# Four graph layers on one core: x added in layer 4, large counts searched where A is made, the flag read between the layers

## The chip, the core and the metric

The kernel runs on one core of one Trainium2 chip. The metric is the time of one execution on the device in microseconds; the median of the runs counts. A core has these engines: PE (TensorE, with its weight loads shown apart as PEld), DVE (VectorE), ACT (ScalarE), POOL (GpSimd) and SP (SyncE), and 16 DMA engines that carry what SP, ACT and POOL issue. PE writes its results to PSUM, from which DVE and ACT read them.

## The reference

x has 6250 rows of 256. There are 100,000 edges, sorted by destination, and the destinations crowd at the low rows (6250 times the square of a uniform number); sources are uniform.

```python
h = jnp.maximum(_layernorm(x, axis=-1), 0.0)
# one network of four graph layers (h[src] summed or maximised over dst):
h = _sage_mean(h, ...)   # h @ W1_self + mean(h[src]) @ W1_neigh + b1        (256 -> 512)
h = _sage_pool(h, ...)   # h @ W2_self + max(relu(h @ W2_pool + b)[src]) @ W2_neigh + b2
h = _sage_gcn(h, ...)    # (sum(h[src]) + h) / (deg + 1) @ W3_neigh + b3
h = _sage_mean(h, ...)   # h @ W4_self + mean(h[src]) @ W4_neigh + b4
out = x + (h @ W_fc + b_fc)
```

## The kernel before

**Tiles.** The 6250 rows are 49 tiles of 128 (the last has 106). The first 18 tiles, where most edges end, are "hub" tiles (`HUB = (8, 16, 18)`: 8 are hubs in layer 1, 16 in layer 3, 18 in layer 4). For a hub tile d the kernel makes a matrix A of counts (128 sources x 49 source tiles x 128 destinations, stored as fp8 in the table tab_a), and its sum over edges is then a dense product of A with the whole source table. For the other tiles the edges are gathered in order, 128 rows at a time, and summed by products with one-hot matrices. Tables hold float32 values as three bfloat16 parts (hi, mid, lo), so that each product is three matmuls.

**Making A** (`build`). A tile has 16 windows of 8 destinations, 288 windows in all. For each group of 128 edges of a window, ACT makes a one-hot hs of the source row (L303, L305), DVE a one-hot hm of source tile and destination (L307), and PE adds their product into a PSUM bank pb of 392 columns (L313; 781 products, two banks). After the last group ACT copies the bank to A as fp8 (L317), and after 16 windows SP stores A to tab_a. The first 8 tiles are made in layer 1, where `sums` steps through its list; tiles 8 to 15 are made in the loop of layer 2 up to its step 250, tiles 16 and 17 after that.

**Layer 2** is a loop over 782 steps: POOL gathers 128 rows of tab_p (L1137), DVE takes a running maximum along the sorted edges (L1142), SP stores the runs. Between the steps the loop advances the making of A, early products for layer 3, and `done2`, which ends a tile of layer 2 (L1076, L1080) and stores its rows to tab_r. A scheduler sets the order on each engine from the program's dependences.

**Layers 3 and 4** have the same form: `sums` walks the groups of edges of the tiles that are no hubs (POOL gathers into ring, L379; DVE makes one-hots, L375; PE pg, L397; DVE accumulates, L414 and L416), and between the steps advances a list of dense products for the hub tiles (`dense`, PE pd, L435). Their A arrives in chunks of up to seven source tiles through `stream`: ACT's queue issues the loads ac (L1214), four ahead, in five buffers. A tile that is finished is handed to `done3` or `done4`, generators that `sums` steps, one step per 128 edges.

`done3` makes q = (sum + own row) / (deg + 1) + a constant row, with 512 columns (the weights that follow are already in the table's values): the first 256 are all that layer 4 needs of the row itself, the last 256 are what layer 4 sums over edges. The last 256 are split into three parts (`parts`, L280 to L283: ACT, DVE, ACT, DVE) and stored to tab_s. The first 256 are added to the rows of x, which ACT's queue has loaded (xrf), and stored to the table xq (L1280 and the line after it).

`done4` loads its tile of xq on ACT's queue (xr4, three buffers, L1303), DVE adds the sum times 1/deg (L1305), SP stores to out (L1307).

**The check and the flag.** A count of 16 or more must not go unseen: in layer 4, `stream` is called with check set, and after each load of ac DVE compares the chunk with 16, sums the hits in the same instruction (L1219) and keeps the maximum in a column of bad (L1221). Together with other checks of the input, bad is reduced after layer 4 (worst, L59), summed over the rows by PE (L63), made an integer (oddI, L67) and read into a register on all engines; if it isn't zero, a general version of the whole computation runs. It isn't run on this input.

Of the kernel before, what the change touches and what calls it, by code (L numbers as in the profile page):

```python
# [9 lines left out]
F32 = mybir.dt.float32  # L10
BF16 = mybir.dt.bfloat16
# [4 lines left out]
ALU = mybir.AluOpType  # L16
AX = mybir.AxisListType
PSUM = bass.MemoryType.PSUM
DRAM = bass.MemoryType.DRAM

P = 128
# [28 lines left out]
@with_exitstack  # L50
def kernel(ctx, tc, *aps):
    nc = tc.nc
    keep = ctx.enter_context(tc.tile_pool(name="keep", bufs=1))
    bad = keep.tile([P, 8 + MERGED], F32, name="bad")
    nc.vector.memset(bad, 0.0)
    fast_path(tc, bad, *aps)
    with tc.tile_pool(name="fl", bufs=1) as fp, tc.tile_pool(name="flp", bufs=1, space=PSUM) as pp:
        worst = fp.tile([P, 1], F32, name="worst")
        nc.vector.tensor_reduce(worst, bad, AX.X, ALU.max)  # L59
        ones = fp.tile([P, P], F32, name="ones_f")  # L60
        nc.vector.memset(ones, 1.0)
        pw = pp.tile([P, 1], F32, name="pw_f")
        nc.tensor.matmul(pw, ones, worst, start=True, stop=True)  # L63
        odd = fp.tile([P, 1], F32, name="odd")
        nc.vector.tensor_scalar(odd, pw, 1.0, None, op0=ALU.min)
        oddI = fp.tile([P, 1], I32, name="oddI")
        nc.vector.tensor_copy(oddI, odd)  # L67
        general = nc.values_load(oddI[:1, :1], min_val=0, max_val=1)
    with tc.If(general > 0):
        general_path(tc, *aps)  # L70


@with_exitstack
def fast_path(
    ctx, tc, bad, x, src, dst,
    W1_self, W1_neigh, b1, W2_pool, b2_pool, W2_self, W2_neigh, b2,
    W3_neigh, b3, W4_self, W4_neigh, b4, W_fc, b_fc, out,
):
# [11 lines left out]
    nc = tc.nc  # L90
# [115 lines left out]
    nc.vector.memset(one, 1.0)  # L206
    first_p = const.tile([P, P], F32, name="first_p")
    nc.vector.tensor_scalar(first_p, pidx.to_broadcast([P, P]), 0.0, None, op0=ALU.is_equal)

    lim = const.tile([1, 4, NT], F32, name="lim")  # L210

# [79 lines left out]
    def build(d, A, keys, pool, psb):  # L291

        sk, mk, r0 = keys
        work = []
        for w in range(d * WT, (d + 1) * WT):
            hold = {}
            for k in range(k_of[w]):
                r = row_of[w, k] - r0
                hots = {}

                def hot(r=r, hots=hots):
                    t = pool.tile([P, P], BF16, name="ht", bufs=3)
                    nc.scalar.activation(t, iota_b, AF.Abs, bias=sk[:, r : r + 1])  # L303
                    hots[0] = pool.tile([P, P], BF16, name="hs", bufs=LOOK + 3)
                    nc.scalar.activation(hots[0], t, AF.Relu, bias=one, scale=-1.0)  # L305
                    hots[1] = pool.tile([P, NT * WIN], BF16, name="hm", bufs=LOOK + 3)
                    nc.vector.tensor_scalar(hots[1], iota_w, mk[:, r : r + 1], None,  # L307
                                            op0=ALU.is_equal)

                def run(k=k, w=w, hots=hots, hold=hold):  # L310
                    if k == 0:
                        hold[0] = bank(psb, "pb", "pb", (NT * WIN,))
                    nc.tensor.matmul(hold[0], hots[0], hots[1], start=(k == 0),  # L313
                                     stop=(k == k_of[w] - 1))
                    if k == k_of[w] - 1:
                        c = (w % WT) * WIN
                        nc.scalar.copy(A[:, :, c : c + WIN],  # L317
                                       hold[0].rearrange("p (s c) -> p s c", c=WIN),
                                       saturate=True)
                        if w % WT == WT - 1:  # L320
                            nc.sync.dma_start(tab_a[d], A.bitcast(BF16))

                work.append((hot, run))
        return work
# [614 lines left out]
    with tc.tile_pool(name="fl2c", bufs=1) as ck, ExitStack() as late:  # L939
# [259 lines left out]
                    now.remove(g)  # L1199
        early.advance(len(early.work))  # L1200


    def stream(pool, chunks, check):

        got = {}
        where = {(d, s): i for i, (d, s0, s1) in enumerate(chunks) for s in range(s0, s1)}

        def load(i):
            if i >= len(chunks):
                return  # L1210
            d, s0, s1 = chunks[i]
            got[i] = pool.tile([P, 7, P], F8, name="ac", bufs=5)
            t = got[i][:, : s1 - s0, :]
            nc.scalar.dma_start(t.bitcast(BF16), tab_a[d, :, s0:s1, :])  # L1214
            if check:

                m = pool.tile([P, 1], F32, name="am")
                many = pool.tile([P, 7, P], BF16, name="many", bufs=1)
                nc.vector.tensor_scalar(many[:, : s1 - s0, :], t, 16.0, 0.0, op0=ALU.is_ge,  # L1219
                                        op1=ALU.add, accum_out=m)  # L1220
                nc.vector.tensor_tensor(bad[:, 3:4], bad[:, 3:4], m, op=ALU.max)  # L1221

        for i in range(4):
            load(i)

        def block(d, s):
            i = where[d, s]
            if s == chunks[i][1]:
                load(i + 4)
            return got[i][:, s - chunks[i][1], :]  # L1230

        return block
# [7 lines left out]
    with ExitStack() as on:  # L1240
# [8 lines left out]
        with tc.tile_pool(name="fl3", bufs=2) as wk:  # L1249
            def done3(d, acc):  # L1250
                q = wk.tile([P, FH], F32, name="q", bufs=2)
                if d < H3:
                    nc.vector.tensor_add(q, acc, acc3[d])
                    nc.vector.scalar_tensor_tensor(q, q, rgcn[:, d : d + 1], qrow,
                                                   op0=ALU.mult, op1=ALU.add)
                else:
                    if d in Z3:
                        z = Z3[d]
                    else:
                        z = wk.tile([P, 3 * FH], BF16, name="zown", bufs=2)  # L1260
                        nc.sync.dma_start(z, tab_r[d * P : (d + 1) * P, :])
                        yield 1
                        yield 1
                        yield 1
                    own = bank(psm, "pm", "pm_own")
                    for part in range(3):
                        nc.tensor.matmul(own, ident_b, z[:, part * FH : (part + 1) * FH],  # L1267
                                         start=(part == 0), stop=(part == 2))
                    yield 1
                    nc.vector.tensor_add(acc, acc, own)  # L1270
                    nc.vector.scalar_tensor_tensor(q, acc, rgcn[:, d : d + 1], qrow,
                                                   op0=ALU.mult, op1=ALU.add)
                n = P if d < NFULL else NREM
                xr = wk.tile([P, FI], F32, name="xrf")
                nc.scalar.dma_start(xr[:n, :], x[d * P : d * P + n, :])
                q3 = wk.tile([P, 3 * FO], BF16, name="q3")
                parts(q[:, FO:], FO, q3)
                nc.sync.dma_start(tab_s[d * P : (d + 1) * P, :], q3)
                yield 1
                nc.vector.tensor_add(xr[:n, :], xr[:n, :], q[:n, :FO])  # L1280
                nc.sync.dma_start(xq[d * P : d * P + n, :], xr[:n, :])
                yield 1
                for s0, s1 in z4_early:
                    if d == s1 - 1:
                        Z4.update(resident(zk, tab_s, FO, s0, s1))
# [2 lines left out]
            Z3 = {}  # L1288
            for s0, s1 in late:
                Z3.update(resident(wk, tab_r, FH, s0, s1))  # L1290
            block = stream(wk, [(d, s0, s1) for d in range(H3) for s0, s1 in late], False)
            todo = []
            work = []
            for d in range(H3):
# [1 line left out]
                              lambda acc, d=d: todo.append(done3(d, acc)))  # L1296
            sums(wk, psg, tab_r, FH, srcE, keyE, jb, H3, done3, 7, Hub(work), wait=14, todo=todo)

        with tc.tile_pool(name="fl4", bufs=2) as wk:
            def done4(d, acc):  # L1300
                n = P if d < NFULL else NREM
                xr = wk.tile([P, FI], F32, name="xr4", bufs=3)
                nc.scalar.dma_start(xr[:n, :], xq[d * P : d * P + n, :])  # L1303
                yield 1
                nc.vector.scalar_tensor_tensor(xr[:n, :], acc[:n, :], rmean[:n, d : d + 1],  # L1305
                                               xr[:n, :], op0=ALU.mult, op1=ALU.add)
                nc.sync.dma_start(out[d * P : d * P + n, :], xr[:n, :])  # L1307
# [1 line left out]
            for s0, s1 in z4_late:  # L1309
                Z4.update(resident(wk, tab_s, FO, s0, s1))  # L1310
            order = [*z4_early, *z4_late]
            block = stream(wk, [(d, s0, s1) for d in range(H4) for s0, s1 in order], True)
            todo = []
            work = []
            for d in range(H4):
# [647 lines left out]
```

## Time and profile before

| what | value |
|---|---|
| three runs | 3079.99, 3082.79, 3087.31 us (median 3082.79) |
| the profiled execution | 3087.14 us, its span 3085.3 us |
| granted TensorE clock, mean | 0.907 |
| PE, DVE, POOL, ACT busy | 80%, 67%, 67%, 29% |
| searches for large counts (L1219, with its read of the accumulator, and L1221) | 144 times, 138.7 + 11.8 + 22.9 us of DVE |
| A copies (L317) | 288 times, 139.8 us of ACT |

Stages by the trace, in us of the span: preparation to 135; layer 1 to about 800; layer 2 to about 2137; layer 3 to 2637; layer 4 to 3065; flag and end to 3085.3. The page's 40 slices (each 77 us; tenths of busy time) show the stages:

```profile
PE   1568999999768555666789997972899899799997
DVE  4955666655367677555789997974466667576665
ACT  2557766664255566311111111000000001000000
PEclk9777999999889777788899998985999999899999
DMA  5454667776599999999989998976999999777774
```

PE is full in layer 1 (slices 4 to 10), the transfers in most of layer 2 and in layer 3, DVE in late layer 2 (slices 21 to 24). In views of waits, a line names who waited, what came last, the total, how often, and the longest wait; waits of an engine that isn't late itself cost nothing. In the chain of waits each piece is what the next one waited for.

### The profile page before, as it was taken

What the parts mean: (1) busy time and instruction counts of PE and PEld (TensorE: products, weight loads), DVE (VectorE), ACT (ScalarE), POOL (GpSimd) and SP (SyncE); (2) the same over time, 40 slices, a digit from 0 to 9 for tenths busy, and PEclk for the clock granted to TensorE, in tenths of its full rate; (3) what the DMA queues carried; (4) which work ended last, traced back from release to release, by engine and by line L of the source; (5) the groups of instructions that cost most, each with busy time, mean ns of one, the idle gap of its engine ahead of it and who ended that gap; (6) DMA issues with size and microseconds to landing.
All of it is one profiled execution on the core that took longest, in us unless ns stands there. A gap on an engine that the chain in (4) does not pass through costs nothing. (4 is left out here: it accounts for less than half of the span.)

```text
span 3085.3 us, 41397 instructions
## 1 busy us (share of the span) xinstructions
PE 2456.4 (80%) x12699; PEld 1401.4 (45%) x12699; DVE 2053.6 (67%) x5303; ACT 893.7 (29%) x2383; POOL 2054.0 (67%) x2260
## 2 busy tenths in 40 slices
PE   1568999999768555666789997972899899799997
PEld 0234666666433222232334443431344344688786
DVE  4955666655367677555789997974466667576665
ACT  2557766664255566311111111000000001000000
POOL 5274777776366776777667777764676677677663
PEclk9777999999889777788899998985999999899999
DMA  5454667776599999999989998976999999777774
GB/s 190 152 159 138 203 208 211 213 217 211 196 392 376 362 388 352 362 389 384 314 274 324 315 309 296 323 248 210 361 387 373 364 386 382 254 225 219 208 210 135
DMA packets 379984, 865.38 MB, mean 280 GB/s; under 512 B 58064, under 2 KB 151202, under 8 KB 379720
## 3 DMA queue, kind: packets, MB, share of 16 engines
q0 software_dynamic: 146560, 514.74, 50.7%
q1 hardware_dynamic: 175108, 292.47, 25.6%
q10 hardware_dynamic: 58084, 55.44, 5.6%
q8 instruction: 103, 1.69, 0.2%
q14 instruction: 129, 1.06, 0.1%
HBM read 610.65 MB, written 252.58 MB: 280 GB/s over the span
## 5 line engine op out<-in xcount | busy, mean ns | idle before, releaser
L1137 POOL DMA_INDIRECT X<-tab_p,srcIf x782 | 842.3, 1077 | 368.6 <-issue 170.5
L397 PE MATMUL pg<-ring,hot 128*128 128x256 bf16 (+2 forms) x3390 | 685.9, 311 | 96.2 <-DMA ring<-tab_h,srcT 36.5
L435 PE MATMUL pd<-zt,ac 128*128 128x256 bf16 (+1 forms) x3462 | 569.9, 300 | 36.3 <-DMA ac<-tab_a 31.1
L379 POOL DMA_INDIRECT ring<-tab_h,srcT x474 | 450.7, 951 | 194.3 <-PE pg L397 72.2
L397 PEld LDWEIGHTS <-hot 128*128 128x128 bf16 x3390 | 334.2, 99 | 332.1 <-issue 163.4
L435 PE MATMUL pd<-r,ae 128*128 128x512 bf16 x1536 | 383.4, 399 | 102.9 <-DVE acc L934 46.9
L379 POOL DMA_INDIRECT ring<-tab_r,srcE x342 | 333.0, 974 | 162.2 <-PE pg L397 72.5
L435 PEld LDWEIGHTS <-ac 128*128 128x128 fp8e4 x3462 | 338.8, 98 | 171.3 <-DMA ac<-tab_a 23.9
L379 POOL DMA_INDIRECT ring<-tab_s,srcE x314 | 297.7, 948 | 130.2 <-PE pg L397 49.4
L1142 DVE SCALAR_TENSOR_TENSOR X<-X,samef,X 128x512 f32<-128x512 f32 x385 | 288.3, 749 | 133.2 <-DMA X<-tab_p,srcIf 90.9
L416 DVE SCALAR_TENSOR_TENSOR acc<-pg,M,acc 128x257 f32<-128x257 f32 (+2 forms) x518 | 274.7, 561 | 150.6 <-PE pg L397 150.3
L1142 DVE SCALAR_TENSOR_TENSOR X<-X,samef 128x512 f32<-128x512 f32 x391 | 293.1, 750 | 114.2 <-DMA X<-tab_p,srcIf 108.0
L313 PE MATMUL pb<-hm,hs 128*128 128x392 bf16 x781 | 256.2, 376 | 132.4 <-ACT A L317 66.4
L305 ACT ACTIVATE hs<-ht,onef 128x128 bf16<-128x128 bf16 x781 | 290.2, 395 | 240.9 <-PE pb L313 221.9
L435 PEld LDWEIGHTS <-ae 128*128 128x128 fp8e4 x1536 | 156.4, 102 | 338.9 <-issue 198.8
L1219 DVE TENSOR_SCALAR_CACHE_REDUCE many<-ac 128x896 bf16<-128x896 fp8e4 (+2 forms) x144 | 138.7, 963 | 132.7 <-DMA ac<-tab_a 132.7
L1076 PE MATMUL pm_prf<-unf,hTf 128*128 128x512 f32 x392 | 203.9, 647 | 16.6 <-ACT hTf L1067 16.6
L375 DVE TENSOR_SCALAR hot<-iota_bf,keyE 128x128 bf16<-128x128 bf16 x656 | 151.2, 274 | 72.5 <-PE pg L397 65.4
L307 DVE TENSOR_SCALAR hm<-iota_w,mk 128x392 bf16<-128x392 f16 x461 | 155.2, 344 | 56.7 <-PE pb L313 55.0
L317 ACT ACTIVATE A<-pb 128x392 fp8e4<-128x392 f32 x288 | 139.8, 489 | 182.0 <-PE pb L313 137.7
L435 PE MATMUL pd<-Z,A 128*128 128x256 bf16 (+1 forms) x1176 | 187.4, 274 | 0.2
L313 PEld LDWEIGHTS <-hs 128*128 128x128 bf16 x781 | 81.4, 105 | 217.7 <-issue 89.2
(288 smaller groups left out, 2908.1 us busy)
## 6 DMA issues: line engine op xcount, KB each, us to landing
runb<-X SPq DMA_DIRECT2D x208, 512.0 KB
runb<-X SPq DMA_DIRECT2D x183, 256.0 KB
tab_r<-r SPq DMA_DIRECT2D x49, 384.0 KB
tab_a<-A SPq DMA_DIRECT2D x18, 784.0 KB
tab_t<-th SPq DMA_DIRECT2D x49, 256.0 KB
tab_p<-hpf SPq DMA_DIRECT2D x49, 256.0 KB
th<-tab_t ACTq DMA_DIRECT2D x49, 256.0 KB
X<-tab_p,srcIf POOLq DMA_INDIRECT x782
```

The source lines that it names most:

```text
L305: nc.scalar.activation(hots[0], t, AF.Relu, bias=one, scale=-1.0)
L307: nc.vector.tensor_scalar(hots[1], iota_w, mk[:, r : r + 1], None, op0=ALU.is_equal)
L313: nc.tensor.matmul(hold[0], hots[0], hots[1], start=(k == 0), stop=(k == k_of[w] - 1))
L317: nc.scalar.copy(A[:, :, c : c + WIN], hold[0].rearrange("p (s c) -> p s c", c=WIN), saturate=True)
L375: nc.vector.tensor_scalar(hot[j], iota_b, keyT[:, j - jb : j - jb + 1], None, op0=ALU.is_equal)
L379: nc.gpsimd.indirect_dma_start(out=ring[:, j % deep, : 3 * F], out_offset=None, in_=table, in_offset=bass.IndirectOffsetOnAxis(ap=srcT[:, ...
L397: nc.tensor.matmul(pg[:, : F + c], hot[j], X[:, part * F : (part + 1) * F + c], start=(k == 0 and part == 2), stop=(k == n - 1 and part == 1),
L416: nc.vector.scalar_tensor_tensor(acc[d], pg, m, acc[d], op0=ALU.mult, op1=ALU.add)
L435: nc.tensor.matmul(hold[0][:, : F + c], a, z[:, part * F : (part + 1) * F + c], start=(s == ss[0] and part == 2), stop=(s == ss[-1] and pa ...
L1076: nc.tensor.matmul(pm, hT[:, c, :], un[:, c, :], start=False, stop=(c == KH - 1))
L1137: nc.gpsimd.indirect_dma_start(out=X[:, k, :], out_offset=None, in_=tab_p, in_offset=bass.IndirectOffsetOnAxis(ap=srcI[:, t : t + 1], axis=0),
L1142: nc.vector.scalar_tensor_tensor(X[:, k, :], prev, same[:, t : t + 1], X[:, k, :], op0=ALU.mult, op1=ALU.max,)
```

## The change

Three things are changed. The search for large counts moves from the chunks of A in layer 4 to the place where A is made: DVE takes the maximum of each window's PSUM bank (a column of the new tile most per window, 288 in all), and at the end of layer 2 these are reduced and compared with 16. x is no longer loaded and added in layer 3: q's first half goes to xq as it is, and layer 4 loads x and xq and adds them on DVE; `done4` has two steps more between the loads and the add. The operations behind the flag become the function `settle`, which is called between layers 3 and 4 and has its tiles in the pools that layers 3 and 4 share (its PSUM tile is a bank beside their 2 + 3 + 2).

```diff
-    fast_path(tc, bad, *aps)
-    with tc.tile_pool(name="fl", bufs=1) as fp, tc.tile_pool(name="flp", bufs=1, space=PSUM) as pp:
+    flag = []
+
+    def settle(fp, pp):
+
         worst = fp.tile([P, 1], F32, name="worst")
         nc.vector.tensor_reduce(worst, bad, AX.X, ALU.max)
...
-        general = nc.values_load(oddI[:1, :1], min_val=0, max_val=1)
+        flag.append(nc.values_load(oddI[:1, :1], min_val=0, max_val=1))
+
+    fast_path(tc, bad, settle, *aps)
+    general = flag[0]
     with tc.If(general > 0):
         general_path(tc, *aps)
...
+    most = const.tile([P, NW], F32, name="most")
...
                     if k == k_of[w] - 1:
                         c = (w % WT) * WIN
+                        nc.vector.tensor_reduce(most[:, w : w + 1], hold[0], AX.X, ALU.max)
                         nc.scalar.copy(A[:, :, c : c + WIN],
...
         early.advance(len(early.work))
-
-    def stream(pool, chunks, check):
+        nc.vector.tensor_reduce(bad[:, 3:4], most, AX.X, ALU.max)
+        nc.vector.tensor_scalar(bad[:, 3:4], bad[:, 3:4], 16.0, None, op0=ALU.is_ge)
+
+    def stream(pool, chunks):
...
             nc.scalar.dma_start(t.bitcast(BF16), tab_a[d, :, s0:s1, :])
-            if check:
-
-                m = pool.tile([P, 1], F32, name="am")
-                many = pool.tile([P, 7, P], BF16, name="many", bufs=1)
-                nc.vector.tensor_scalar(many[:, : s1 - s0, :], t, 16.0, 0.0, op0=ALU.is_ge,
-                                        op1=ALU.add, accum_out=m)
-                nc.vector.tensor_tensor(bad[:, 3:4], bad[:, 3:4], m, op=ALU.max)
...
-                n = P if d < NFULL else NREM
-                xr = wk.tile([P, FI], F32, name="xrf")
-                nc.scalar.dma_start(xr[:n, :], x[d * P : d * P + n, :])
                 q3 = wk.tile([P, 3 * FO], BF16, name="q3")
                 parts(q[:, FO:], FO, q3)
                 nc.sync.dma_start(tab_s[d * P : (d + 1) * P, :], q3)
-                yield 1
-                nc.vector.tensor_add(xr[:n, :], xr[:n, :], q[:n, :FO])
-                nc.sync.dma_start(xq[d * P : d * P + n, :], xr[:n, :])
+                nc.sync.dma_start(xq[d * P : (d + 1) * P, :], q[:, :FO])
                 yield 1
...
+        settle(zk, on.enter_context(tc.tile_pool(name="flp", bufs=1, space=PSUM)))
         with tc.tile_pool(name="fl4", bufs=2) as wk:
             def done4(d, acc):
                 n = P if d < NFULL else NREM
                 xr = wk.tile([P, FI], F32, name="xr4", bufs=3)
-                nc.scalar.dma_start(xr[:n, :], xq[d * P : d * P + n, :])
+                nc.scalar.dma_start(xr[:n, :], x[d * P : d * P + n, :])
+                q = wk.tile([P, FO], F32, name="q4", bufs=3)
+                nc.scalar.dma_start(q[:n, :], xq[d * P : d * P + n, :])
                 yield 1
+                yield 1
+                yield 1
+                nc.vector.tensor_add(xr[:n, :], xr[:n, :], q[:n, :])
                 nc.vector.scalar_tensor_tensor(xr[:n, :], acc[:n, :], rmean[:n, d : d + 1],
                                                xr[:n, :], op0=ALU.mult, op1=ALU.add)
```

The calls of `stream` lose their last argument.

More of the change, by code (lines that the diff above doesn't have):

```diff
@@ L74, in fast_path @@
 def fast_path(
-    ctx, tc, bad, x, src, dst,
+    ctx, tc, bad, settle, x, src, dst,
     W1_self, W1_neigh, b1, W2_pool, b2_pool, W2_self, W2_neigh, b2,
@@ L1290, in fast_path @@
                 Z3.update(resident(wk, tab_r, FH, s0, s1))
-            block = stream(wk, [(d, s0, s1) for d in range(H3) for s0, s1 in late], False)
+            block = stream(wk, [(d, s0, s1) for d in range(H3) for s0, s1 in late])
             todo = []
@@ L1311, in fast_path @@
             order = [*z4_early, *z4_late]
-            block = stream(wk, [(d, s0, s1) for d in range(H4) for s0, s1 in order], True)
+            block = stream(wk, [(d, s0, s1) for d in range(H4) for s0, s1 in order])
             todo = []
```

## The prediction

> **What bounds the kernel now.** I read the 40 slices first: no engine is full throughout, so the kernel is a row of stages with different limits. I therefore took busy times by stretch, then the waits and the chain inside the stretches that the change touches. Columns below: stretch, length, then busy us (and instructions) of PE, PEld, DVE, ACT and POOL, granted clock, DMA share, GB/s.
>
> ```profile
> 300.00:790.00 490.00, 473.41 (x3181) 323.44 (x3179) 286.98 (x1048) 311.40 (x829) 356.43 (x375) 1.00 0.69 208
> 830.00:1300.00 470.00, 306.21 (x887) 146.82 (x887) 314.91 (x755) 256.27 (x752) 320.29 (x306) 0.80 1.00 372
> 1580.00:1860.00 280.00, 264.07 (x1022) 120.48 (x1021) 263.93 (x410) 50.38 (x111) 213.31 (x193) 0.99 0.94 315
> 2300.00:2450.00 150.00, 132.94 (x599) 58.62 (x597) 91.51 (x229) 11.34 (x28) 102.22 (x105) 0.98 1.00 379
> 2637.00:3065.00 428.00, 399.34 (x3587) 351.30 (x3588) 286.29 (x962) 0.00 (x0) 297.36 (x314) 0.98 0.74 221
> ```
>
> Layer 1 (first row) is PE: 473 of 490 us. Early layer 2 is the transfers (1.00), with DVE at 67%. Late layer 2 is DVE and PE together (94% each). Layer 3 is the transfers again (1.00). Layer 4 is PE: 399 of 428 us, so at most 28.7 us can be won there. The A copies, counted by line L317 in the first three stretches (ACT busy and count), say where the new work falls:
>
> ```profile
> 300.00:790.00 490.00, 53.10 (x109) 1.00 0.69 208
> 830.00:1300.00 470.00, 63.24 (x131) 0.80 1.00 372
> 1580.00:1860.00 280.00, 7.06 (x15) 0.99 0.94 315
> ```
>
> The waits of layer 4 (2637 to 3065), as waiting line, what came last, us in total, times, longest, and then two of layer 3 (2150 to 2637):
>
> ```profile
> DVE many L1219 <- DMA ac<-tab_a: 132.7, 44, 5.3
> ...
> PE pd L435 <- DMA ac<-tab_a: 31.1, 18, 12.1
> ```
> ```profile
> DVE q L281 <- ACT q L280: 60.9, 17, 17.0
> ACT q L280 <- DMA xq<-xrf: 58.6, 8, 22.7
> ```
>
> PE loses 31.1 us to ac, of which the longest, 12.1, is the start of the layer (it ends at 2639.25); 19.0 us are 17 waits inside it. The critical chain of 2790 to 2820 shows how these arise:
>
> ```profile
> 2790.07 1.00 DVE many L1219 x2
> ...
> 2791.49 3.19 DMA out<-xr
> ...
> 2795.17 3.85 DMA ac<-tab_a
> ```
>
> DVE's order holds the last sum of a tile (L1305) behind a search for large counts, the search waits for ac, the ac loads stand on ACT's queue behind the xr load, and that waits for the out store three tiles back (xr4 has 3 buffers). A circle, in which DVE's searches are one link.
>
> **Layer 4: the searches leave.** Gone are 144 x (963 + 82 + 159 ns) = 138.7 + 11.8 + 22.9 = 173.4 us of DVE work. DVE has 142 us to spare there, so not this sum but PE's waits count. The circle is loosened, not cut: the x load still waits for the out store three back, with the q load and ac loads behind it, but the sums come as soon as PE is done. The new add (128x256, 0.42 us by L1280) waits for x and q, and stands about four hots (5.2 us) after the previous out store was issued, while store and load need 3.2 + 0.4 + 4.2 = about 8 us: DVE will stand some 2.8 us per tile with hots and accs queued behind, but hots run six steps (8 us) ahead of PE. From 19.0 us of mid-waits I take 14 back (about three in four, the rest staying with the out store's own 3 us and more), less 1 us at the start, where x and q loads stand between the ac loads: -13. Bounds: all of them, -19; nothing back and 4 lost at the start, +4.
>
> The Trainium skill speaks against the second load: "DMA: Bandwidth & Descriptors", section "Issuing engines are not separate DMA queues", says that transfers run on the same 16 engines whichever engine issues them. By the row it is cheap here: the stretch's share is 0.74, and one more 128 KB load per tile adds about what the xr loads take, 4.7 points, to 0.79. By the rule alone 48 x 128 KB = 6.3 MB at the 221 GB/s seen would be +28 us. I go by the row, since 0.26 of the engines' time is free; but the same rule is why the load's leaving helps layer 3.
>
> **Layer 3: x leaves.** The 1 KB packets of ACT's queue there are the x loads, 3.9% of 16 engines over 2200 to 2600, where the share is 0.996: 15.5 us. With them go 48 adds (20.3 us of DVE, not on the path) and the wait of ACT's queue on the xq store of two tiles back, which holds ACT's next split (58.6 us in 8 waits) and then DVE (60.9 in 17); of this PE saw 8.56 us at 2449 and 2.2 at 2526. The xq store stays, now from q itself (2 buffers); a q is rewritten 6.5 us or more after its store was issued, the store lands in 5 to 7 and twice in 18 to 22, so this new hold shows at most twice. I take -13; bounds -18 (load and PE's waits) and -4 (only a quarter, the gathers' own latency remaining).
>
> **Layers 1 and 2: 288 reductions are added.** Each reads 128x392 float32 in PSUM. Nearest rows:
>
> ```profile
> L416 DVE SCALAR_TENSOR_TENSOR acc<-pg,M,acc 128x257 f32<-128x257 f32 x215 | 95.8, 481 | 112.0 <-PE pg L397 111.7
> ...
> L639 DVE TENSOR_REDUCE bad<-hasw 1x1 f32<-1x288 f32 x1 | 0.4, 433 | 0.0
> ```
>
> With 512 columns L416 takes 746 ns, so 1.04 ns a column: 0.62 us for 392. The reduction of 288 took 433 ns, at 1.0 ns a column 0.54. I take 0.6 us, 173 us in all (156 to 179): as much as layer 4 loses. The skill ("VectorE: DVE Perf Modes", section "Rules for kernel authors") calls tensor_reduce DVE's slowest operation, always at 1x; the rows agree, and cost it no more than any PSUM read.
>
> What matters more is the order. The skill's "PSUM — Partial Sum Buffer", section "PSUM bank collisions raise a hardware error", says two engines may not read one bank at once; the instruction order of the changed kernel obeys, ACT's A copy (489 ns) now waiting on the reduction in nearly all of 288 cases. So PE, then DVE, then ACT, then PE again (two pb banks; L313 already waits 66.4 us for the copy). By the rows side by side nothing but 0.6 us of DVE would be spent; by the rule each window holds its bank 0.6 us longer plus whatever DVE is waiting on.
>
> Layer 1: 128 windows, one per 4.5 us, DVE 59% busy; banks are not short, but the last window of each of 8 tiles delays that tile's store by 0.6, and PE has no slack: +4 (0 to 10).
> Early layer 2: 131 windows in 470 us, 79 us on top of 315: DVE rises to 84%, still under the transfers, and 12 X buffers take up the jitter. PE has 164 us idle. +5 (0 to 35: half of the reductions paid whole, 39, is about the top).
> Late layer 2 (1500 to 1900): DVE 94% busy, no cover; some 22 windows of which 18 in the full part, x 0.6 = +10 (5 to 15).
>
> **The flag.** In the order, the four small DVE operations and PE's product are put where DVE and PE end layer 2, not behind layer 3, and only SP's register load moves there, ahead of the last tab_r store; the other engines' loads stay at the end. SP then waits for oddI: 1.1 us on the boundary, where the tab_r store (2139.64) starts layer 3: +1 (0 to 2). At the end the chain worst, ones, pw, odd, oddI (3068.5 to 3069.7) is gone and PE's branch (4.36 us) starts earlier: -2 (-1 to -4). The final reduction over 288 columns is 0.43 us, in the +1.
>
> **Sum.** +4 + 5 + 10 + 1 - 13 - 13 - 2 = -8 us. The profiled execution took 3087.1 (span 3085.3), 4.3 over the median of 3082.8; the profile forecast is 3079, the median 3082.8 - 8 = **3075**.
>
> **Rivals.** *A, the reductions are covered*: layer 1 nothing, early layer 2 nothing, late 5; layer 4 gives 18: 0 + 0 + 5 + 1 - 13 - 18 - 2 = -27, **3056**. For it: DVE idle in 33% of early layer 2. Against: 94% later.
> *B, the wait on ac stays*: x load, q load and ac still stand behind the out store, so layer 4 gives 0 in place of -13 (and the same time if layer 3 gives none): +5, **3088**. For it: DMA pieces are over 60% of that chain, the searches 23%.
> *C, the reduction ties three engines in early layer 2*: it stands in DVE's order behind X steps that wait for gathers (198.9 us in 202 waits over the layer), ACT's copy and its next hs wait for it, and PE for those. If 40% of 131 are paid whole, 31 us in place of 5: +18, **3101**. It decides from 19 us in that stretch, where the sum passes +6. For it: gathers queue on X buffers that DVE frees. Against: 33% idle DVE and 35% idle PE there.
>
> **Numbers.** Measurement tells 0.2%, 6.2 us, from no change. Forecast (3066 to 3084) 0.40, A 0.17, B 0.20, C 0.23. A lies below 3076.6 whole, over half of the forecast too, a little of B where half of a gain comes: faster 0.46. Same: the rest of the forecast and most of B, 0.27. Slower: C and B's upper end, 0.27. The range goes from 3050 (below A: layer 3 at -18) to 3104 (C with half of the reductions).
>
> **What would show it.** L1219 and L1221 gone; a most row of 288 at 540 to 620 ns; if 800 or more, late layer 2 loses more. Stage ends: layer 2 from 2137 to about 2157, layer 3 from 492 us to about 479, layer 4 from 428 to 415. PE's mid-waits on ac under 8 us (B: still 15 or more). DMA share in layer 4 near 0.79. In 830 to 1300, X waits on gathers shrink and the stretch's same count of X steps takes under 10 us more (C: 20 or more). The forecast is wrong if X steps wait for reductions, or if the granted clock (0.907 over the run) changes with the denser work.

## The result, and the profile after

The changed kernel takes 3041.47 us (median of 4 runs, 3032.44 to 3044.61), the kernel before beside it 3085.05 (4 runs). The ratio is 0.986, 95% interval 0.9831 to 0.9888: some 43 us faster where 8 were forecast, and below the low end of the range (3050). Run once more it was 0.9857 (0.9836 to 0.9878). Of the six sets of runs here, each beside the kernel before, two had that kernel at about 3485 us instead of 3085 to 3091, for a reason that no trace here shows, and most of the change gained nothing there (flag_end, below, 1.0029), so their ratios stand in a column of their own and the conclusions rest on the other sets.

The profiled execution took 3044.6 us (span 3042.8), 42.5 less than that of before. The granted TensorE clock, whose change the prediction named as a sign of being wrong, is 0.909 where it was 0.907. The same stretches as shown of before (busy us of PE, PEld, DVE, ACT, POOL; granted clock; DMA share), the last one being layer 4 again, which now begins at about 2618:

```profile
300.00:790.00 490.00, 474.18 (x3160) 322.20 (x3159) 328.92 (x1155) 312.59 (x829) 358.62 (x377) 1.00 0.70 209
830.00:1300.00 470.00, 321.48 (x911) 153.12 (x912) 367.77 (x882) 272.50 (x768) 317.17 (x302) 0.79 1.00 367
1580.00:1860.00 280.00, 243.42 (x946) 110.59 (x944) 263.77 (x421) 51.03 (x112) 210.90 (x192) 0.97 0.95 317
2300.00:2450.00 150.00, 143.55 (x655) 63.48 (x654) 101.86 (x244) 12.94 (x32) 109.00 (x114) 1.00 1.02 392
2625.00:3034.00 409.00, 395.87 (x3572) 350.87 (x3573) 168.61 (x575) 0.00 (x0) 296.85 (x312) 0.98 0.82 247
```

Layer 1 is unchanged but for 42 us of DVE work more that costs it next to nothing. Layer 3's row has PE at 96% (143.6 of 150) where it had 89%: the transfers are as full as before, but bring more gathers. Layer 4 has DVE at 41% instead of 67%, DMA at 0.82 instead of 0.74, and PE at 97%. The waits of layer 4, in the columns of before:

```profile
DVE xr L1308 <- DMA xr<-in_x: 133.7, 35, 7.7
...
PE pd L442 <- DMA ac<-tab_a: 12.2, 5, 9.8
```

PE's 19.0 us of waits in mid-layer are 2.4 (12.2 less the start's 9.8). DVE now stands 133.7 us at the new add, and little follows from it: in the same stretch as before (2790 to 2820) the chain that ends last runs through PE alone, of which this is the start:

```profile
2789.94 0.98 PE pd L442 x9
2790.92 0.33 PE pg L404 x3
2791.25 0.98 PE pd L442 x9
2792.23 0.33 PE pg L404 x3
```

The reductions, and the add, by form:

```profile
L323 DVE TENSOR_REDUCE most<-pb 128x1 f32<-128x392 f32 x288 | 160.8, 559 | 32.6 <-PE pb L319 31.9
L1308 DVE TENSOR_TENSOR xr<-xr,q 128x256 f32<-128x256 f32 x48 | 20.5, 429 | 160.7 <-DMA xr<-in_x 130.6 <-issue 13.8 <-DMA ac<-tab_a 11.6
```

Read off at the same six events in each trace (first, 201st and 301st maximum step X of layer 2 by DVE, the last prf of done2, the last q of layer 3, the last sum of layer 4), stage lengths in us are as follows. Kernels that are explained further down stand beside them.

| trace | to layer 2 | X 0 to 200 | X 200 to 300 | rest of layer 2 | layer 3 | layer 4 | end | span |
|---|---|---|---|---|---|---|---|---|
| before | 827.9 | 324.2 | 177.3 | 807.4 | 493.1 | 438.6 | 16.9 | 3085.3 |
| after | 831.4 | 343.0 | 166.4 | 801.9 | 475.1 | 419.1 | 6.0 | 3042.8 |
| after_again | 830.4 | 346.1 | 167.8 | 801.1 | 476.6 | 419.6 | 6.0 | 3047.6 |
| x_only_b | 829.7 | 329.3 | 176.9 | 813.1 | 477.6 | 488.1 | 17.1 | 3131.9 |
| search_only_b | 828.9 | 345.9 | 167.6 | 796.6 | 494.7 | 412.3 | 17.5 | 3063.5 |
| flag_end_b | 831.9 | 345.8 | 167.4 | 802.2 | 481.5 | 416.2 | 17.4 | 3062.4 |
| no_search | 828.6 | 325.1 | 175.3 | 808.9 | 490.7 | 413.5 | 16.9 | 3059.1 |
| no_reduce_b | 828.5 | 323.8 | 175.2 | 814.0 | 477.6 | 416.8 | 7.6 | 3043.5 |
| pool_late | 829.6 | 343.0 | 165.5 | 800.2 | 474.8 | 416.3 | 15.4 | 3044.7 |
| reduce_after_copy | 832.0 | 336.8 | 167.7 | 796.5 | 473.8 | 415.4 | 6.0 | 3028.3 |
| reduce_after_copy_c | 830.0 | 343.9 | 165.2 | 792.7 | 476.1 | 420.6 | 6.0 | 3034.4 |
| x_only_deep_c | 829.4 | 328.3 | 174.8 | 807.9 | 475.7 | 488.0 | 16.8 | 3121.0 |

After less before: +3.5, +18.8, -10.9, -5.5, -18.0, -19.5, -10.9, together -42.5 us. Each row is one execution, and two traces of the same kernel (after, after_again) differ by up to 3.1 us in a stage.

### The profile page after: what moved, and what is told of

The parts are those of the page before. It is cut to its first block, busy times and chain, and to the rows that moved or that the text cites. A ratio compares the mean times of both kernels' runs of the same rounds, so it can differ in the third digit from the quotient of the medians.

```text
span 3042.8 us, 41553 instructions
## 1 busy us (share of the span) xinstructions
PE 2459.1 (81%) x12699; PEld 1402.3 (46%) x12699; DVE 2039.5 (67%) x5161; ACT 905.7 (30%) x2383; POOL 2051.3 (67%) x2260
## 5 line engine op out<-in xcount | busy, mean ns | idle before, releaser
L442 PE MATMUL pd<-zt,ac 128*128 128x256 bf16 (+1 forms) x3462 | 566.8, 299 | 21.6 <-DMA ac<-tab_a 12.2
L323 DVE TENSOR_REDUCE most<-pb 128x1 f32<-128x392 f32 x288 | 160.8, 559 | 32.6 <-PE pb L319 31.9
```

What stands on the lines that cost most here:

```text
L323: nc.vector.tensor_reduce(most[:, w : w + 1], hold[0], AX.X, ALU.max)
L442: nc.tensor.matmul(hold[0][:, : F + c], a, z[:, part * F : (part + 1) * F + c], start=(s == ss[0] and part == 2), stop=(s == ss[-1] and pa ...
```

## The experiments

Theory P is the prediction with its sizes; theory M takes the sizes from the two traces: layers 1 and 2 about +6, layer 3 -18, layer 4 -15 to -20, the end -9 to -11.

| kernel | ratio (interval), beside 3085 to 3091 | ratio (interval), beside 3485 |
|---|---|---|
| after_again | 0.9857 (0.9836 to 0.9878) | |
| x_only, x_only_b | 1.0125 (1.0091 to 1.0159) | 0.9989 (0.9965 to 1.0013) |
| search_only, search_only_b | 0.9937 (0.9915 to 0.9959) | 1.0034 (1.0006 to 1.0062) |
| flag_end, flag_end_b | 0.9872 (0.9838 to 0.9905) | 1.0029 (1.0004 to 1.0054) |
| no_reduce, no_reduce_b | 0.9860 (0.9826 to 0.9895) | 0.9959 (0.9936 to 0.9983) |
| no_search | 0.9911 (0.9892 to 0.9929) | |
| pool_late, pool_late_b | 0.9870 (0.9849 to 0.9891) | 1.0059 (1.0032 to 1.0085) |
| reduce_after_copy, _c, _b | 0.9820 (0.9802 to 0.9837), 0.9831 (0.9804 to 0.9858) | 0.9960 (0.9933 to 0.9986) |
| x_only_deep_c, x_only_deep | 1.0116 (1.0087 to 1.0146) | 1.0003 (0.9976 to 1.0029) |
| copy_first_deep | | 0.9973 (0.9950 to 0.9996) |

### x alone

The kernel before with the x part of the change, and nothing else. The main lines (the load of xrf, the new add and the steps of the generators change with them, as in the changed kernel):

```diff
-                nc.vector.tensor_add(xr[:n, :], xr[:n, :], q[:n, :FO])
-                nc.sync.dma_start(xq[d * P : d * P + n, :], xr[:n, :])
+                nc.sync.dma_start(xq[d * P : (d + 1) * P, :], q[:, :FO])
...
-                nc.scalar.dma_start(xr[:n, :], xq[d * P : d * P + n, :])
+                nc.scalar.dma_start(xr[:n, :], x[d * P : d * P + n, :])
+                q = wk.tile([P, FO], F32, name="q4", bufs=3)
+                nc.scalar.dma_start(q[:n, :], xq[d * P : d * P + n, :])
```

> The kernel before with only the adding of x moved to layer 4; the search for large counts and the flag stay as they were. Theory P (the sizes of the prediction): layer 3 gains 13 us, layer 4 with its searches gains nothing and may lose up to 4, so -9 to -13 us against the kernel before. Theory M (the sizes that the two traces show): layer 3 with its start gains 18, layer 4 with its searches 0 to -4, so -14 to -18. A third theory, that x and the search only pay together since layer 4 can't carry a second load beside the searches: layer 4 loses 10 or more, so -8 or less.

> The first four kernels ran on a chip on which PE stood 42 us in layer 4 for nothing that the profile shows, so they are run again, hoping for the chip of the second four. x_only: theory M gives layer 3 -16 to -18 (as the changed kernel's two traces) and layer 4, which keeps its searches, 0 to +6 for the second load (no_search's layer 4 is 413.5 us long, the changed kernel's 419), so -10 to -18 against the kernel before. Theory P: -9 to -13. If x can only move because the searches leave, layer 4 loses 10 and more: -8 or less.

x_only_b cost 1.25%, some 39 us, where both theories had it faster (x_only, 0.9989, shows no difference). Only the third theory, a layer 4 that can't carry the load beside the searches, has the right sign, and its size was far too small. Layer 3 does gain 15.5 us (18.0 in the changed kernel); layer 4 takes 49.5 us longer. Its waits:

```profile
DVE xr L1304 <- DMA xr<-in_x: 85.7, 39, 6.2
DVE many L1219 <- DMA ac<-tab_a: 72.6, 44, 4.6
PE pd L435 <- DMA ac<-tab_a: 59.8, 29, 9.8
```

The add waits for x on DVE in both kernels. Here the searches stand behind it in DVE's order, an ac buffer is free only when it is searched, and PE waits for ac 59.8 us, where it waited 31.1 before and 12.2 after. Over the whole of layer 4 PE stands 74.5 us instead of 38.9, and its 3588 products take 14.0 us more, at a granted clock of 0.95 instead of 0.97. The chain that ends last can be followed here from 3032 us on; a piece of it shows one round:

```profile
3071.79 1.00 DVE many L1219 x2
...
3073.45 3.54 DMA out<-xr
...
3077.52 3.57 DMA ac<-tab_a
3081.11 1.09 DVE many L1219 x2
...
3086.13 2.43 DMA xr<-in_x
...
3088.66 0.42 DVE xr L1304
...
3089.46 5.55 DMA ac<-tab_a
3095.03 1.09 DVE many L1219 x2
3096.13 0.40 DVE xr L1305
...
3096.55 1.70 DMA out<-xr
...
3098.35 2.05 DMA xr<-in_x
```

Sums (L1305) stand between the searches, the out store follows the sum, ACT's queue issues the next x load when that store has landed and the ac load behind it, and the next search waits for that ac. No engine is short of time in this layer: the DMA engines are busy for a share of 0.71 (0.82 in the changed kernel, which has the same two loads) and DVE for 64%. That it is the order that costs the time, and not DVE's work as such, is argued from these shares and the chain; no run changes the order alone.

### The search alone, and no search at all

search_only is the kernel before with the reductions in `build` and without the comparisons in `stream`; no_search has the comparisons taken out and nothing in their place, so large counts are not looked for.

> The kernel before with only the search for large counts moved to where A is made; x is still added in layer 3 and the flag is read at the end. Theory P: +4 +5 +10 in layers 1 and 2 and -13 in layer 4, so about +6 us. Theory M: +6 in layers 1 and 2 (last tile of layer 2 ends 6 us later than before) and -15 to -20 in layer 4, so -9 to -14.

> no_search measured -28 against the kernel before, all of it in layer 4; with the 288 reductions added, theory M: +3 to +6, so -22 to -25; theory P: +19, so -9. If it is as on the first chip (+12), the chip had no part in it.

> The kernel before without any search for large counts (this part of the check is left out), x in layer 3, the flag at the end. It shows what layer 4 alone wins when the searches go. Theory P: -13 us, since the loads of ac still stand behind the xr load that waits for the out store. Theory M: -17 to -20, PE's mid-waits on ac under 3 us. Against search_only it is the price of the 288 reductions without the moved x: 19 by P, 6 by M.

no_search is 0.9911 (27 us) and its layer 4 is 25.1 us shorter, more than M's 17 to 20 and nearly all of the 28.7 that PE had to win; search_only is 0.9937 (19 us). So P, which gave layer 4 13, is out. The searches alone were layer 4's trouble: with them gone, PE has no wait for ac in mid-layer that this profile lists. The moved x then costs layer 4 3 to 4 us (flag_end_b 416.2 and no_reduce_b 416.8 against 412.3 and 413.5) instead of 49.5, and layer 3 wins its 13 (481.5 against 494.7, and 477.6 against 490.7). The two parts aren't a sum: +1.25% and -0.63% apart, -1.28% together in flag_end_b.

### The reductions

no_reduce is the changed kernel without L323; the search is left out.

> The changed kernel without the 288 reductions: large counts are not looked for at all (this part of the check is left out). Theory P: layers 1 and 2 give back 19 us against the changed kernel (4 + 5 + 10). Theory M: the traces give them 6 us, so -4 to -8. A third theory, that the reductions cost 19 and something else in layer 2 went faster by 13 in that one execution, would show as -15 or more with the last tile of layer 2 ending near 2123.

> The changed kernel without the reductions and so without the search (left out), against the changed kernel's -43: theory P gives them 19, so -62; theory M 3 to 6, so -46 to -49. A third theory, from reduce_after_copy (-57): the reductions themselves cost nothing or less, since they pull making of A and the ends of tiles into the part of layer 2 in which DVE has time, and only ACT's wait behind them costs: then -43 or less gain.

no_reduce_b is 0.9860, the changed kernel 0.9857 to 0.986: net the reductions cost nothing within 13 us, so P's 19 is too much; the pair search_only_b and no_search gives 8, within 9. In the other column no_reduce is 0.9959 where flag_end is 1.0029, the early flag included in the difference.

The stage table says where the net comes from. In every trace with reductions the first 200 X steps take 337 to 346 us, in every one without 324 to 329. But X step 200 lies in the middle of the making of A: with reductions 102 or 103 windows are made in these 200 steps, without them 91 or 92, and steps 200 to 300 are then shorter, 165 to 168 us against 175 to 177. Over the first 300 steps, in which 133 windows are made either way, the reductions cost 9.5 us (511.6 in the mean of the five traces with the reduction ahead of the copy, 502.1 in the five without), and the rest of layer 2 is 9.9 us shorter (800.4 against 810.3).

The shorter rest is not in its last part: from step 501 on, layer 2 takes 476 us in before and after alike, though the changed kernel has 14 reductions (7.8 us) there. DVE is busy 399.9 and 399.7 us in it, since five early adds (L934), one done2 and two hm fewer are left to do; PE is busy 361.4 us instead of 383.6. In every trace with reductions here, 82 to 84 of the 1536 early products for layer 3 stand before step 300, and none without. So the making of A, the ends of tiles and the early products stand earlier against the X steps: the early stretch pays, and what comes later is paid back. That this order is what pays back is argued: no run has the reductions in the old order.

The next experiment keeps the reductions and swaps them with ACT's copy:

```diff
-                        nc.vector.tensor_reduce(most[:, w : w + 1], hold[0], AX.X, ALU.max)
                         nc.scalar.copy(A[:, :, c : c + WIN],
...
                                        saturate=True)
+                        nc.vector.tensor_reduce(most[:, w : w + 1], hold[0], AX.X, ALU.max)
```

> The changed kernel with each reduction behind ACT's copy of the same bank instead of ahead of it: ACT waits for PE alone, and PE's next use of the bank waits for DVE. If the serial order PE, DVE, ACT costs something in layers 1 and 2 (P: some 5 us of early layer 2, more if DVE stands in its queue), this gives -3 to -8 against the changed kernel, or a loss if PE's next product then waits longer for DVE than it did for ACT. If the order doesn't matter (M), within 3 us.

> The kernel with the reduction behind ACT's copy once more. It was 0.982 of before, the changed kernel 0.9857 beside it. If ACT's wait for DVE is what it saves: 0.980 to 0.984 again. If it was one chip's chance: 0.986.

> 0.982 of before the first time, the changed kernel twice 0.986; 0.996 on the slower chip, where flag_end was 1.003. If ACT's wait for DVE is what it saves: 0.980 to 0.984. If the first was chance: 0.986.

0.9820 and 0.9831, 8 to 11 us below the changed kernel, and faster than both kernels: the best version found. The first interval ends just below that of the changed kernel beside it (0.9836 to 0.9878); the run in another set agrees. The gain lies in layer 2, which takes 1301 and 1302 us in the two traces, and 1309 to 1315 in the five with the reduction ahead of the copy. There (820 to 2140) the changed kernel has these waits:

```profile
PE pb L319 <- ACT A L324: 109.4, 63, 7.6
ACT A L324 <- DVE most L323: 83.9, 53, 9.4
```

and with the copy first

```profile
PE pb L319 <- DVE most L326: 103.8, 54, 7.2
```

PE waits for its bank about as long either way; what goes is ACT's 83.9 us behind DVE, and with it the delay of what ACT does next. That this is the cause of the 8 to 11 us is argued, not shown: no run takes ACT's wait alone.

### The flag

flag_end is the changed kernel with the flag's operations and loads at the end, as before. pool_late leaves the flag early and adds one POOL instruction that needs the last tile, so that POOL's own load, branch and drain come at the end:

```diff
                 nc.sync.dma_start(out[d * P : d * P + n, :], xr[:n, :])
+                if d == NT - 1:
+                    last = zk.tile([P, 1], F32, name="last")
+                    nc.gpsimd.tensor_copy(last[:n, :], xr[:n, :1])
```

> The changed kernel with the flag's operations and its registers put back to the end. Theory P: the early flag is worth 1 us, so +1 against the changed kernel. Theory M: in the trace of before POOL's drain (7.43 us, 3077.07 to 3084.50) starts only after its register load and branch and sets the end; in the changed kernel POOL has loaded the register at 3018.5 after its last gather and drains under the work of the others. So +9 to +11 against the changed kernel, and from the last sum to the end of the span about 16.8 us as before, where the changed kernel has 6.0.

> The changed kernel with the flag at the end, against the changed kernel's -43 on the second chip: theory M (10.8 us between last sum and end in the traces) -32 to -35; theory P (1 us) -42. pool_late's median came out only 2 us over the changed kernel although its profile has the drain at the end, 15.4 us after the last sum; if that median is right, -41.

> The changed kernel with one POOL instruction added that reads one column of the last tile's sum: POOL's register load, branch and drain can then start only at the end, while the flag's five small operations stay at the end of layer 2 and the other engines' order is the changed kernel's. Theory P (what the early flag saves is the chain worst to oddI and PE's branch): 0 to +1 us against the changed kernel. Theory M (it is POOL's drain of 7.4 us that comes off the end): +7 to +10, the whole of what the early flag is worth.

> The changed kernel with POOL's register load, branch and drain held to the end, once more. Theory M: +9 against the changed kernel's 0.986, so 0.989; if the early flag's worth is hidden otherwise: 0.986 to 0.987 as measured the first time.

The traces agree with M. From the last sum to the end: 16.9 us before, 6.0 after, 17.4 with the flag at the end, and 15.4 in pool_late, where everything of the flag but POOL's part is early. So 9.4 of the 10.9 us are POOL's. What stands there isn't counted as busy on the page; the trace's records of before, start and us:

```
3069.93  1.184  POOL  TENSOR_LOAD   oddI
3075.05  1.995  POOL  INC_SWDGE_SEM
3077.07  7.427  POOL  DRAIN
3084.55         POOL  last semaphores
```

In the changed kernel POOL loads the register at 3018.46, as soon as its last gather is issued, drains from 3025.52 to 3032.95 while the others work, and the last sum ends at 3036.8. The medians say less: flag_end_b is 0.0015 above the changed kernel and pool_late 0.0013, 4 to 5 us, with intervals of 9 to 12 that hold both 0 and M's 9. pool_late_b (1.0059) has no changed kernel beside it to be compared with. So the end is shown by the traces, its worth in the median only bounded.

### Deeper buffers

x_only once more with six buffers for xr4 and q4 instead of three; and copy_first_deep, the same on reduce_after_copy.

> x_only with six buffers for xr4 and q4 in layer 4 instead of three, searches still in layer 4. If the loss of x_only's layer 4 (+49 us in its trace) is the circle in which the x load waits for the out store three tiles back, DVE's add for the load, the searches for DVE and the next sum for the searches, the deeper buffers cut it: -5 to -20 against the kernel before. If it is DVE's work or the second load's share of the transfers, it stays at +25 to +40.

> On a chip where the kernel before takes about 3085 us, x_only was 1.0125 of it. With six buffers for xr4 and q4: 0.994 to 0.998 if the circle of three buffers is what cost it 49 us in layer 4; 1.008 to 1.013 if it is DVE's work or the second load's share. On the slower chip it was 1.0003, and x_only 0.9989 there.

> The reduction behind ACT's copy, and six buffers for xr4 and q4. PE's mid-waits on ac in layer 4 are down to 2.4 us in the changed kernel and its start (9.8) isn't touched by this, so at most -3 to -5 against reduce_after_copy_b, if DVE's standing at the add (133.7 us in 35 waits) costs nothing; if that standing does hold PE, -10.

The expectation of a gain failed: x_only_deep_c is 1.0116, and layer 4 is 488.0 us as with three buffers. The trace tells why this isn't a verdict on the circle. With three buffers, x load n is issued 2 to 7.5 us after out store n-3 was (in x_only_b and in the changed kernel); with six, 2 to 6 us after out store n-6; and q load n is issued 0.4 us after the end of add n-3 or, from the sixth on, n-6. The order puts each load as early as its buffer comes free, and the add behind the load, mostly 41 to 61 us ahead of the sum that needs it (mostly 11 to 29 with three buffers). So ACT's queue and DVE stand as before, only for a later tile: DVE waits 86.9 us for x where it waited 85.7. What would take the circle apart, loads on another queue or an add placed late, wasn't tried. copy_first_deep (0.9973) can't be told from reduce_after_copy_b (0.9960).

## Why the prediction was wrong, point by point

**Direction** was right, the sum (-8 us) much too small (-43). Of the 34.5 us between the forecast and the traces' -42.5, 12.6 lie in layer 2, 8.9 at the end, 6.5 in layer 4, 6 in layer 3 with its start and 0.5 in layer 1. The steps:

- *The reduction, 0.6 us, 173 in all*: right, 559 ns, 161 us.
- *Layer 1, +4*: +3.5 in that trace, about +2 over all; right.
- *Early layer 2, +5 (0 to 35)*: the steps that stood between 830 and 1300 us take 9.7 us more, within the range and under the 10 that was named for it (15.0 in after_again). The +18.8 of X 0 to 200 is in part the making of A, moved ahead of step 200.
- *Late layer 2, "no cover", +10*: this step failed most. From step 300 on layer 2 is 5.5 shorter (9.9 in the means), and its last 476 us are as long as before with 14 reductions in them. The reductions were priced on top of an order taken as fixed; the order had moved, and the order of the changed kernel was there to be compared. All of layer 2 costs 2.4, not 15.
- *Layer 3, -13, and boundary +1*: -18.0 in this pair, 16 in the means of the traces with and without x in layer 3. Both terms of the bound (-18) show: the 15.5 us of transfers went, and DVE's wait for the split went from 60.9 us to 13.6, PE's wait for gathers from 33.3 to 16.6.
- *Layer 4, -13*: -19.5. The mechanism held: PE's mid-waits fell by 16.6 where 14 were forecast, the start got 2.3 shorter instead of 1 longer, and DVE's standing at the add did not hold PE (forecast 2.8 us a tile, measured 3.8 in 35 waits). But "a circle, in which DVE's searches are one link" sized it too low: without them layer 4 wins 25.1 (no_search), and the new load takes 3 to 4 back.
- *The second load by the row, 0.74 to 0.79*: the share rose to 0.82, which is the 0.79 of 428 us in the 409 that were left; in the changed kernel the row was the right guide, and the 28 us by the rule alone were not paid. But the row prices transfers; x alone cost 49.5 us while the engines' share was 0.71. The prediction had no term for that, since it priced both parts together.
- *The flag, -2*: -10.9. The chain worst to oddI and PE's branch were counted; POOL's 2.0 and 7.43 us behind its branch, in the trace of before, were put at nothing, although they end last. "The other engines' loads stay at the end" was true of the order only: POOL's stands behind its last gather, and with the flag ready nothing holds it there.

**Rivals.** A, at 3056, was the nearest; with the end at -10.9 instead of -2 it would have said 3047. Its 18 us from layer 4 and its reductions without a net price were right, its parts in layer 2 were not: nothing early (+7.8 over 300 steps) and 5 late (-5.5) came out near the truth only together, by luck. B is out: PE's mid-waits on ac are 2.4 us, and its sign was 15 or more. C's 31 us in early layer 2, or the 19 from which it decides, did not come: 9.7, and 15.0 in after_again.

## What to carry to other kernels

Price an edit against the order that it makes, not against the old one: compare what stands in each stretch before adding the new work to it, since what is moved out can be worth as much. What a scheduler hoists to a free buffer kept waiting here with three buffers as with six. A check that stands in an engine's order costs what waits behind it: the same load cost 49.5 us beside the searches and 3 to 4 without. Cut a stretch where the same work is done on both sides: at step 200 the reductions seemed to cost 18.8 us, at step 300 7.8. At a kernel's end, follow every engine to its last record, the ones not counted as busy too.

## What the runs showed of the hardware

POOL, which issues gathers in all these kernels, ends with a drain of 7.43 us and 2.0 us ahead of it, in each trace here. In before they end last; in the changed kernel, where POOL begins the drain 11 us ahead of the last sum, they cost nothing.

A maximum over 128x392 float32 in PSUM took DVE 559 ns. By the rows of before, 481 ns for a scalar_tensor_tensor over 257 columns of PSUM and 746 over 512, such an operation would take 621 at 392 columns, an estimate: the maximum is no dearer.
